# Layer 0's last head pair: the root by POOL's power, value copies on ScalarE, and rows turned only between two tiles of a projection job

## The chip, the cores and the metric

The kernel runs on one NeuronCore of a Trainium2 chip. The metric is the time of one execution on the device in microseconds (us). A core has five engines with instruction streams of their own: TensorE (PE) for matmuls and transposes, with its weight loads shown apart as PEld; VectorE (DVE); ScalarE (ACT), whose functions come from tables that are loaded when they change; GpSimd (POOL); and SyncE (SP), which here issues the DMA transfers. Each engine takes its instructions strictly in order and waits on semaphores for the others. On-chip memory is SBUF, and PSUM for the results of matmuls.

## The reference

Two layers over N = 4096 nodes with 512 features, 8 heads of 64, in float32. Layer 0 is graph attention with additive scores, layer 1 attention with dot products:

```python
h = relu(layernorm(x))                       # layer 0
d1 = (h @ W.T + b).reshape(N, 8, 64)
src, trg = (d1 * src_proj).sum(-1), (d1 * trg_proj).sum(-1)
e = leaky(src.T[:, :, None] + trg.T[:, None, :]) + adj     # slope 0.01
x = x + (softmax(e) @ d1 per head)
h = relu(layernorm(x))                       # layer 1
k, q, v = h @ Wks, h @ Wqs, h @ Wvs          # per head
s = q @ k.T / 8 - 1e16 * (1 - max(adj, eye))
x = x + sum over heads of softmax(s) @ v @ Wo
```

The layer norm of layer 1 needs all 512 features of a row, and so the sums of all of layer 0's heads.

## The kernel before, in words

The program has three stages. Stage A does the first three head pairs of layer 0 with tiles of 128 rows by 4096 columns. Stage B, from about 1717 us to 2529 us of the span, does the last pair. Stage C is layer 1. The change touches stage B alone, apart from one constant (`neghalf`) made at the start.

Stage B works in **slots**, the loop over `s` at its end. A slot handles 32 rows by 4096 columns for both heads of the pair, laid out as 128 partitions by 1024 columns for each head: a partition holds one row and a quarter of the columns. Four slots (`GS`) make a **group** of 128 rows, and there are 32 groups, so 128 slots. Two groups (`BR`) make a **block** of 256 rows. The order of the instructions on each engine is the order of the program, since the stage stands under `manual_schedule`. For one slot's data the steps are spread over several passes of the loop:

- the adjacency rows are loaded three slots ahead by SP (L586, four DMAs of 128 KB);
- `leaky(s+1)` (L599, ACT): source plus target score through the leaky function, into one of two PSUM buffers per head tile (`lk`);
- `masked(s)` (L609, DVE, twice): adds the adjacency, writes the negated sum to the SBUF ring `t` and takes the row's smallest value. The ring has 12 slots (`RING`), so three groups;
- `parted` (L616, POOL) and, in every even slot, `smallest` (L625 on PE into the single PSUM buffer `ms`, L630 on DVE): the smallest values of a row's four quarters brought together;
- `exps(s-3)` (L641, ACT, twice): the exponentials with their sums;
- `squares(s-4)` (L648, DVE): transposes 32x32 squares in place;
- `weighted(s-8)` (L656, PE, 32 matmuls, here called the output pass): sums a quarter of the columns times the values d1 for all four slots of a group into the PSUM tile `bo`. Four such passes finish a group.

A group's results then pass through `finish`, a generator that is advanced once per slot: den (L672, PE) and its reciprocal (L676, DVE) in one slot, back (L680, PE, transposing the group's output that ACT copied with L665) and batt (L682, DVE) two slots later, then the addition to the residual row tile on POOL (L686), the statistics on DVE (L690, L694), and for every second group the root on ACT (L700), its reciprocal on DVE (L702), the normalisation on POOL (L706), and the transposes of the two row tiles on PE (L716, called turns), each with its relu on DVE (L717). The finished block is handed to `projected`, a **job**: queries and keys for layer 1, four PSUM tiles copied out by ACT (L733), and values, two PSUM tiles copied out by DVE (L745); each copy goes to HBM through SP.

In detail, a job has 32 query and key units, eight for each of the four tiles, and eight value units, four for each of the two tiles; in PE's timeline a unit is two matmul instructions. `work` runs in each slot and spends `UNITS` credits on the job at the head of the list: a query or key unit counts one, a value unit two, so that a job costs 48. PE's order in a slot is: `work`, `smallest` (even slots), the steps of `finish`, the output pass. ACT's is: copy of a finished group's output (first slot of a group), leaky, exponentials, then the copies of `work`. DVE's is: two masks, squares, what `work` gives it, the minima, the steps of `finish`.

Three bounds tie the engines together. The tiles of the turns and of the projections share one PSUM pool of two buffers (tag `mp`): a tile can begin when the one before the last has been copied out. The ring `t` lets the masks of a group's first slot start only when the output pass of the slot just before it is done. And the output pass of a group's first slot needs the squares of that group's last slot.

After the last slot the remaining jobs run on alone; this part is called the tail. Stage C starts with the keys and values that the jobs wrote.

Of the kernel before, what the change touches and what calls it, by code (L numbers as in the profile page):

```python
# [8 lines left out]
F32 = mybir.dt.float32  # L9
AF = mybir.ActivationFunctionType  # L10
ALU = mybir.AluOpType
# [4 lines left out]
P = 128  # L16
EPS = 1e-5
# [6 lines left out]
def kernel(  # L24
# [14 lines left out]
    nc = tc.nc  # L39
    N, DM = x.shape  # L40
    H, D = src_proj.shape[1:]
    HD = H * D
    NB = N // P
    KC = DM // P
# [6 lines left out]
    const = ctx.enter_context(tc.tile_pool(name="const", bufs=1))  # L51
    dram = ctx.enter_context(tc.tile_pool(name="dram", bufs=1, space=DRAM))

    ident = const.tile([P, P], F32, name="ident")
    make_identity(nc, ident)
    eps = const.tile([P, 1], F32, name="eps")
    nc.gpsimd.memset(eps, EPS)


    SQ = 32  # L60
    NS = P // SQ
    band = const.tile([P, SQ], F32, name="band")
# [36 lines left out]
    with tc.tile_pool(name="a0k", bufs=1) as pk, tc.tile_pool(name="a0v", bufs=4) as pv, tc.tile_pool(  # L99
        name="a0a", bufs=3  # L100
    ) as pa, tc.tile_pool(name="a0t", bufs=6) as pt, tc.tile_pool(name="a0p", bufs=4) as pp, tc.tile_pool(
        name="a0x", bufs=1
    ) as px, tc.tile_pool(name="a0h", bufs=3) as ph, tc.tile_pool(name="a0s", bufs=4) as psb, tc.tile_pool(
        name="a0tr", bufs=3, space=PSUM
# [200 lines left out]
        hTs = [None]  # L305
# [119 lines left out]
        def step(n):  # L425
            return groups[n // 2], n % 2

        with tc.manual_schedule():
# [45 lines left out]
            for s in range(total + 6):  # L474
                G, h = step(s) if s < total else (None, 0)
                for half in range(2):
# [4 lines left out]
                    turn = 0 <= n < 2 * total  # L481
                    if turn:
                        T, i = groups[n // HALVES], n % HALVES
# [43 lines left out]
    RING = 12  # L527
    EXPS, TURN, PROD = 3, 4, 8
    BR = 2
    UNITS = 6  # L530
    with tc.tile_pool(name="b0c", bufs=1) as pc, tc.tile_pool(name="b0a", bufs=4) as pa, tc.tile_pool(
        name="b0w", bufs=1
    ) as pk, tc.tile_pool(name="b0t", bufs=1) as pt, tc.tile_pool(name="b0v", bufs=GS) as pv, tc.tile_pool(
        name="b0x", bufs=6
    ) as pxr, tc.tile_pool(name="b0h", bufs=4) as ph, tc.tile_pool(name="b0e", bufs=4) as pe, tc.tile_pool(
        name="b0ht", bufs=2
    ) as phT, tc.tile_pool(
        name="b0s", bufs=6
    ) as psb, tc.tile_pool(name="b0o", bufs=1) as px, tc.tile_pool(
        name="b0lk", bufs=2, space=PSUM  # L540
    ) as plk, tc.tile_pool(name="b0m", bufs=1, space=PSUM) as pm, tc.tile_pool(
        name="b0po", bufs=1, space=PSUM
# [124 lines left out]
        def finish(G):  # L667

            yield
            den = pm.tile([P, P], F32, tag="ms", name="den")  # L670
            for k in range(GS):
                nc.tensor.matmul(  # L672
                    den[bass.ts(k, SQ), :2], lhsT=band, rhs=G.sm[:, k, :], start=True, stop=True
                )
            rden = psb.tile([P, 2], F32, name="rden")
            nc.vector.reciprocal(rden, den[:, :2])  # L676
            yield
            yield
            back = pm.tile([P, P], F32, tag="ms", name="back")
            nc.tensor.transpose(back, G.oT, ident)  # L680
            att = px.tile([P, 2, D], F32, name="batt")
            nc.vector.tensor_mul(  # L682
                att, back.rearrange("p (h d) -> p h d", d=D), rden.unsqueeze(2).to_broadcast([P, 2, D])
            )
            last = G.x[:, C3 * PR :]
            nc.gpsimd.tensor_add(last, last, att.rearrange("p h d -> p (h d)"))  # L686
            nc.sync.dma_start(x1_d[bass.ts(G.g, P), C3 * PR :], last)
            yield
            stats = psb.tile([P, 6], F32, name="bstats")
            nc.vector.bn_stats(stats, G.x)  # L690
            if G.g % BR == 0:
                block[0] = psb.tile([P, BR, 2], F32, name="bmv")
            mv = block[0]
            nc.vector.bn_aggr(mv[:, G.g % BR], stats)  # L694
            if G.g % BR < BR - 1:
                return
            Gs = groups[G.g - BR + 1 : G.g + 1]
            yield
            rstd = psb.tile([P, BR, 1], F32, name="brstd")
            nc.scalar.activation(rstd, mv[:, :, 1:2], AF.Sqrt, bias=eps)  # L700
            yield
            nc.vector.reciprocal(rstd, rstd)  # L702
            hns = []
            for j in range(BR):
                hn = ph.tile([P, DM], F32, name="bhn")
                nc.gpsimd.tensor_scalar(  # L706
                    hn, Gs[j].x, mv[:, j, 0:1], rstd[:, j], ALU.subtract, ALU.mult
                )
                hns.append(hn)
            yield  # L710
            hT = phT.tile([P, KC, BR * P], F32, name="bhT")
            for j in range(BR):
                yield
                tp = pmm.tile([P, KC, P], F32, tag="mp", name="tp")
                for kc in range(KC):
                    nc.tensor.transpose(tp[:, kc, :], hns[j][:, bass.ts(kc, P)], ident)  # L716
                nc.vector.tensor_scalar(hT[:, :, bass.ts(j, P)], tp, 0.0, None, ALU.max)  # L717
            jobs.append(projected(Gs, hT))

        def projected(Gs, hT):  # L720

            rows = bass.ts(Gs[0].g // BR, BR * P)
            for c in range(HC):
                mp = pmm.tile([P, 2, BR * P], F32, tag="mp", name="mp")
                for i, w in ((0, wk), (1, wq)):
                    for kc in range(KC):
                        nc.tensor.matmul(
                            mp[:, i], lhsT=w[:, kc, bass.ts(c, P)], rhs=hT[:, kc, :],
                            start=(kc == 0), stop=(kc == KC - 1),
                        )  # L730
                        if (i, kc) == (1, KC - 1):
                            e = pe.tile([P, 2, BR * P], F32, name="e")
                            nc.scalar.copy(e, mp)  # L733
                            nc.sync.dma_start(qk_d[:, c, :, rows], e)
                        yield 1
            for j in range(BR):
                mp = pmm.tile([P, 512], F32, tag="mp", name="mpv")
                for kc in range(KC):
                    nc.tensor.matmul(
                        mp, lhsT=hT[:, kc, bass.ts(j, P)], rhs=wv[:, kc, :],  # L740
                        start=(kc == 0), stop=(kc == KC - 1),
                    )
                    if kc == KC - 1:
                        e = pe.tile([P, 512], F32, name="e")
                        nc.vector.tensor_copy(e, mp)  # L745
                        nc.sync.dma_start(v_d[bass.ts(Gs[j].g, P), :], e)
                    yield 2

        groups = [Rows(g) for g in range(NG)]
        block = [None]  # L750
        jobs = []

        def step(n):
            return groups[n // GS], n % GS

        def work():

            units = 0
            while jobs and units < UNITS:
                try:  # L760
                    units += next(jobs[0])
                except StopIteration:
                    jobs.pop(0)

        with tc.manual_schedule():
# [4 lines left out]
            for s in range(SETS + PROD + 10):  # L770
# [23 lines left out]
                if s % 2 and s < SETS:  # L794
                    G, k = step(s)
# [3 lines left out]
                if s % 2 == 0 and 0 <= s - 2 < SETS:  # L799
                    G, k = step(s - 2)  # L800
# [3 lines left out]
                if 0 <= n < SETS:  # L804
                    W, w = step(n)
                    weighted(W, w)
                    if w == GS - 1:
                        endings = [*endings[-2:], finish(W)]
            while jobs:
                work()  # L810
    l0.close()
    att_d = dram.tile([HC, P, N], F32, name="att_d")
# [17 lines left out]
    with tc.tile_pool(name="a1t", bufs=1) as pt, tc.tile_pool(name="a1k", bufs=4) as pkk, tc.tile_pool(  # L830
        name="a1v", bufs=GS
    ) as pv, tc.tile_pool(name="a1a", bufs=6) as pa, tc.tile_pool(name="a1q", bufs=2) as pq, tc.tile_pool(
        name="a1x", bufs=2
    ) as px, tc.tile_pool(name="a1s", bufs=6) as psb, tc.tile_pool(name="a1z", bufs=2) as pz, tc.tile_pool(name="a1at", bufs=3) as pat, tc.tile_pool(
        name="a1sc", bufs=4, space=PSUM
    ) as psc, tc.tile_pool(name="a1tr", bufs=1, space=PSUM) as ptr, tc.tile_pool(
        name="a1m", bufs=1, space=PSUM
# [271 lines left out]
        with tc.manual_schedule():  # L1109
# [18 lines left out]
            for s in range(total + PROD + 3):  # L1128
# [11 lines left out]
                turn = 0 <= s - TURN < total  # L1140
                if turn:
                    squares(*step(s - TURN))
                turn = turn and (s - TURN) % 2
# [3 lines left out]
                if s % 2 and 0 <= s - 3 < total:  # L1147
                    G, k = step(s - 3)
# [16 lines left out]
                if s % 2 and s < total:  # L1165
                    G, k = step(s)
# [46 lines left out]
```

## Time and profile before

| What | Value |
|---|---|
| Median of 3 runs | 4940.27 us (4938.2 to 4942.55) |
| Profiled execution, time | 4940.09 us |
| Profiled execution, span of the core | 4938.3 us |
| Mean granted TensorE clock | 0.98 of full |
| PE, DVE, ACT, POOL busy over the span | 96%, 90%, 78%, 9% |
| Stage B: first leaky, last matmul of the last job ends | 1723.1 us, 2528.9 us |
| One mask (L609), one squares (L648), in ns | 1215, 2307 |
| One leaky (L599), one exponential (L641), in ns | 1113, 1135 |
| Copies L733 (ACT) and L745 (DVE), in ns | 563, 655 |
| Table load, in ns | 1283 |

The span runs from the first to the last instruction of the profiled execution; its time has 1.8 us more around it. In the profile a group of instructions has a line of the kernel, an engine, an operation, and the tiles that it writes and reads. "Idle before" is the time that the engine stood still ahead of these instructions, with what ended it. A releaser is inferred: where the one named had long been done, it was another. A timeline line gives the start in us from the span's start, the length, the engine, the line, and in brackets the wait ahead of it.

### The profile page before, as it was taken

How to read it: one execution, taken by the hardware profiler on the slowest of the kernel's cores; microseconds unless marked ns; L12 is line 12 of the kernel's file. 1: busy time of each engine (PE TensorE's matmuls, PEld its weight loads, DVE VectorE, ACT ScalarE, POOL GpSimd, SP SyncE). 2: the span in 40 equal slices, each digit the busy share in tenths (PEclk: the TensorE clock that was granted, in tenths of full speed). 3: DMA queues.
4: the chain of work that ended last, by engine and by line, in shares of the span. 5: the costliest groups of instructions: out<-in, count | busy, mean ns of one | idle time of the engine just before them, and what ended most of it. 6: DMA issues, size and time to landing. Idle time of an engine off the chain costs nothing.

```text
span 4938.3 us, 144474 instructions
## 1 busy us (share of the span) xinstructions
PE 4719.5 (96%) x61554; PEld 3518.5 (71%) x61554; DVE 4462.5 (90%) x7841; ACT 3857.6 (78%) x4301; POOL 459.2 (9%) x932
## 2 busy tenths in 40 slices
PE   6999999999999958989989999999999999999998
PEld 5888888888888847767756666666666666666664
DVE  4999999999999898888749999999999999999981
ACT  4999999999999899888748888766666666666660
POOL 2000000000000011111123333100000000000000
PEclk8999999999999979999999999999999999999999
DMA  6444454445444384444367787633445343534435
GB/s 233 158 152 157 162 193 161 152 153 206 153 156 158 115 181 135 143 140 135 111 192 249 241 265 237 223 130 131 152 152 170 130 156 129 189 129 136 158 124 192
DMA packets 358838, 819.44 MB, mean 166 GB/s; under 512 B 60080, under 2 KB 179120, under 8 KB 333104
## 3 DMA queue, kind: packets, MB, share of 16 engines
q1 hardware_dynamic: 358192, 810.21, 50.0%
q8 instruction: 481, 7.88, 0.6%
q14 instruction: 165, 1.35, 0.1%
HBM read 669.26 MB, written 140.77 MB: 164 GB/s over the span
## 4 chain that ended last, share of the span: by engine, by line
PE 57%; ACT 15%; DVE 15%; issue 8%; DMA 3%; SPq 1%; POOL 0%; DVEq 0%; ACTq 0%; POOLq 0%
PE sc L920 20%; PE o L1004 20%; ACT t L168 6%; PE tr L986 5%; DVE t L158 5%; DVE pT L192 4%; ACT t L147 4%; DVE bt L609 3%; PE tr L181 3%; PE o L203 3%; ACT pT L190 2%; PE oo L1087 2%; ACT bt L641 2%; DVE bt L648 2%; DMA ba<-in_adj_dram 1%
## 5 line engine op out<-in xcount | busy, mean ns | idle before, releaser
L936 DVE CUSTOM_DVE_ANT_0 t<-sc,a 128x512 f32<-128x512 f32 x2048 | 1285.7, 683 | 99.3 <-PE sc L920 52.0
L971 ACT ACTIVATE t<-t,nm 128x1024 f32<-128x1024 f32 x1024 | 1165.9, 1142 | 103.1 <-DVE nm L960 103.0
L1004 PEld LDWEIGHTS o<-t,v 128*64 128x64 f32 x16384 | 883.8, 137 | 429.4 <-issue 321.2
L920 PE MATMUL sc<-k,q 64*32 64x512 f32 x16384 | 1028.1, 597 | 10.5 <-DVE nm L936 10.4
L1004 PE MATMUL o<-t,v 128*64 128x128 f32 x16384 | 1007.4, 276 | 0.4 <-ACT oT L1013 0.4
L158 DVE CUSTOM_DVE_ANT_0 t<-t,a 128x2048 f32<-128x2048 f32 x384 | 876.0, 2281 | 41.2 <-ACT t L147 41.0
L978 DVE STREAM_TRANSPOSE t<-t 128x1536 f32<-128x1536 f32 x512 | 908.2, 1774 | 1.1 <-ACT t L971 1.1
L181 PE MATMUL tr<-ident,t 128*128 128x128 f32 x6144 | 781.5, 278 | 34.1 <-ACT pT L190 20.1
L203 PE MATMUL o<-pT,v 128*64 128x128 f32 x12288 | 756.8, 276 | 1.0 <-DVE pT L192 0.8
L181 PEld LDWEIGHTS tr<-ident,t 128*128 128x128 f32 x6144 | 665.4, 141 | 125.9 <-issue 65.3
L147 ACT ACTIVATE t<-tb,src 128x4096 f32<-128x4096 f32 x192 | 730.1, 3803 | 18.7 <-DMA tb<-trg_d 18.7
L168 ACT ACTIVATE t<-t,nm 128x4096 f32<-128x4096 f32 x192 | 729.8, 3801 | 8.5 <-DVE nm L163 8.4
L203 PEld LDWEIGHTS o<-pT,v 128*64 128x64 f32 x12288 | 664.0, 137 | 61.3 <-issue 46.8
L993 ACT COPY t<-tr 128x1024 f32<-128x1024 f32 x256 | 259.1, 1012 | 515.9 <-PE tr L986 507.0
L192 DVE COPY pT<-tr 128x1024 f32<-128x1024 f32 x549 | 652.5, 1213 | 9.8 <-PE tr L181 9.8
L920 PEld LDWEIGHTS sc<-k,q 64*32 64x32 f32 x16384 | 259.4, 106 | 371.8 <-issue 215.5
L599 ACT ACTIVATE lk<-tb,srcb 128x1024 f32<-128x1024 f32 x256 | 282.3, 1113 | 82.3 <-DVE nm L609 75.0
L609 DVE CUSTOM_DVE_ANT_0 bt<-lk,ba 128x1024 f32<-128x1024 f32 x256 | 302.0, 1215 | 24.8 <-ACT e L733 12.7
L648 DVE STREAM_TRANSPOSE bt<-bt 128x2048 f32<-128x2048 f32 x128 | 295.2, 2307 | 29.0 <-ACT bt L641 29.0
L641 ACT ACTIVATE bt<-bt,nm 128x1024 f32<-128x1024 f32 x256 | 290.3, 1135 | 0.4 <-DVE nm L630 0.3
L656 PE MATMUL bo<-bt,bv 128*64 128x128 f32 x4096 | 282.8, 297 | 5.9 <-ACT boT L665 4.5
L986 PE MATMUL tr<-ident,t 128*128 128x128 f32 x2048 | 280.8, 280 | 0.8 <-ACT t L971 0.7
(115 smaller groups left out, 3750.5 us busy)
## 6 DMA issues: line engine op xcount, KB each, us to landing
a<-in_adj_dram SPq DMA_DIRECT2D x192, 1024.0 KB
a<-pen_d SPq DMA_DIRECT2D x384, 512.0 KB
ba<-in_adj_dram SPq DMA_DIRECT2D x512, 128.0 KB
a<-in_adj_dram SPq DMA_DIRECT2D x512, 128.0 KB
pen_d<-a SPq DMA_DIRECT2D x128, 512.0 KB
h<-hT_d SPq DMA_DIRECT2D x96, 256.0 KB
qk_d<-e SPq DMA_DIRECT2D x64, 256.0 KB
x<-in_x_dram SPq DMA_DIRECT2D x8, 1024.0 KB
```

The source lines that it names most:

```text
L147: nc.scalar.activation(t, targets[G.c, h], AF.Prelu, bias=src[:, G.g, 2 * G.c + h : 2 * G.c + h + 1], alpha=SLOPE)
L158: nc.vector.tensor_tensor_reduce(out=t, in0=t, in1=rows_of_adj[G, f], scale=-1.0, scalar=FMAX, op0=ALU.add, op1=ALU.min, accum_out=nm[:, f ...
L168: nc.scalar.activation(G.t[h], G.t[h], AF.Exp, bias=G.nm[h][:, NCH : NCH + 1], scale=-1.0, accum_out=G.sm[:, h : h + 1],)
L181: nc.tensor.transpose(tr[:, bass.ts(b % 4 * 2 + h, P)], G.t[h][:, bass.ts(i * MB + b, P)], ident)
L192: nc.vector.tensor_copy(pT, tr)
L203: nc.tensor.matmul(G.o[h * D : (h + 1) * D, :P], lhsT=feats[G.c][i][:, b, bass.ts(h, D)], rhs=pT[:, bass.ts(b % 4 * 2 + h, P)], start=(mb ...
L920: nc.tensor.matmul(sc[h][bass.ts(a, SQ), :], lhsT=G.q[bass.ts(h, D), bass.ds(G.q0 + k * SQ, SQ)], rhs=keys[G.c][half][bass.ts(h, D), a, :] ...
L936: nc.vector.tensor_tensor_reduce(out=t[:, G.ring + k, h, cols], in0=scs[half][h], in1=a[:, cols], scale=1.0, scalar=FMAX, op0=ALU.add, op1 ...
L971: nc.scalar.activation(u, u, AF.Exp, bias=G.nm[k // 2][:, k % 2, h : h + 1], scale=-1.0, accum_out=G.sm[:, h, k : k + 1],)
L978: nc.vector.transpose(u, u)
L986: nc.tensor.transpose(tr[:, j, h, bass.ts(m, P)], t[:, G.ring + k - 1 + j, h, bass.ds(VC + m * P, P)], ident,)
L1004: nc.tensor.matmul(G.o[bass.ts(h, D), :P], lhsT=v[:, b, bass.ts(h, D)], rhs=t[:, bass.ds(G.ring, GS), h, bass.ds(at, SQ)], start=(mb == 0) ...
```

## The change

Six things change in stage B. The root of the variance plus eps is taken on POOL as a power of -0.5 (`neghalf`), with a shift worked out beside it, in place of ACT's Sqrt and DVE's reciprocal, and the normalisation is a multiplication and an addition. The value copies move from DVE to ACT. `den` and `back` share one PSUM tile and come in the same slot, two slots earlier than `back` before. The statistics, the root and the normalisation follow in the next slot. The turns leave `finish`: they stand in a list, and `work` takes one from it only when the job at the head stands between two tiles and fewer than two jobs are listed; after a turn, `work` does no more in that slot. `UNITS` is 7 in place of 6, and credits that a slot leaves are kept, up to 9 in hand.

```diff
--- before.py
+++ after.py
@@ -55,6 +55,8 @@
     make_identity(nc, ident)
     eps = const.tile([P, 1], F32, name="eps")
     nc.gpsimd.memset(eps, EPS)
+    neghalf = const.tile([P, 1], F32, name="neghalf")
+    nc.gpsimd.memset(neghalf, -0.5)
 
 
     SQ = 32
@@ -527,7 +529,7 @@
     RING = 12
     EXPS, TURN, PROD = 3, 4, 8
     BR = 2
-    UNITS = 6
+    UNITS = 7
     with tc.tile_pool(name="b0c", bufs=1) as pc, tc.tile_pool(name="b0a", bufs=4) as pa, tc.tile_pool(
         name="b0w", bufs=1
     ) as pk, tc.tile_pool(name="b0t", bufs=1) as pt, tc.tile_pool(name="b0v", bufs=GS) as pv, tc.tile_pool(
@@ -667,20 +669,17 @@
         def finish(G):
 
             yield
-            den = pm.tile([P, P], F32, tag="ms", name="den")
+            ms = pm.tile([P, 2, P], F32, tag="ms", name="back")
             for k in range(GS):
                 nc.tensor.matmul(
-                    den[bass.ts(k, SQ), :2], lhsT=band, rhs=G.sm[:, k, :], start=True, stop=True
-                )
+                    ms[bass.ts(k, SQ), 1, :2], lhsT=band, rhs=G.sm[:, k, :], start=True, stop=True
+                )
+            nc.tensor.transpose(ms[:, 0], G.oT, ident)
             rden = psb.tile([P, 2], F32, name="rden")
-            nc.vector.reciprocal(rden, den[:, :2])
-            yield
-            yield
-            back = pm.tile([P, P], F32, tag="ms", name="back")
-            nc.tensor.transpose(back, G.oT, ident)
+            nc.vector.reciprocal(rden, ms[:, 1, :2])
             att = px.tile([P, 2, D], F32, name="batt")
             nc.vector.tensor_mul(
-                att, back.rearrange("p (h d) -> p h d", d=D), rden.unsqueeze(2).to_broadcast([P, 2, D])
+                att, ms[:, 0].rearrange("p (h d) -> p h d", d=D), rden.unsqueeze(2).to_broadcast([P, 2, D])
             )
             last = G.x[:, C3 * PR :]
             nc.gpsimd.tensor_add(last, last, att.rearrange("p h d -> p (h d)"))
@@ -695,29 +694,38 @@
             if G.g % BR < BR - 1:
                 return
             Gs = groups[G.g - BR + 1 : G.g + 1]
-            yield
+
             rstd = psb.tile([P, BR, 1], F32, name="brstd")
-            nc.scalar.activation(rstd, mv[:, :, 1:2], AF.Sqrt, bias=eps)
-            yield
-            nc.vector.reciprocal(rstd, rstd)
+            nc.gpsimd.tensor_scalar(rstd, mv[:, :, 1:2], 1.0, EPS, ALU.mult, ALU.add)
+            nc.gpsimd.tensor_tensor(rstd, rstd, neghalf.unsqueeze(1).to_broadcast([P, BR, 1]), ALU.pow)
+            shift = psb.tile([P, BR, 1], F32, name="bshift")
+            nc.gpsimd.tensor_mul(shift, mv[:, :, 0:1], rstd)
+            nc.gpsimd.tensor_scalar(shift, shift, -1.0, 0.0, ALU.mult, ALU.add)
             hns = []
             for j in range(BR):
                 hn = ph.tile([P, DM], F32, name="bhn")
-                nc.gpsimd.tensor_scalar(
-                    hn, Gs[j].x, mv[:, j, 0:1], rstd[:, j], ALU.subtract, ALU.mult
-                )
+                nc.gpsimd.tensor_scalar(hn, Gs[j].x, rstd[:, j], shift[:, j], ALU.mult, ALU.add)
                 hns.append(hn)
             yield
-            hT = phT.tile([P, KC, BR * P], F32, name="bhT")
-            for j in range(BR):
-                yield
+            yield
+            hTs = []
+
+            def turn(j):
+                if j == 0:
+                    hTs.append(phT.tile([P, KC, BR * P], F32, name="bhT"))
+                hT = hTs[0]
                 tp = pmm.tile([P, KC, P], F32, tag="mp", name="tp")
                 for kc in range(KC):
                     nc.tensor.transpose(tp[:, kc, :], hns[j][:, bass.ts(kc, P)], ident)
                 nc.vector.tensor_scalar(hT[:, :, bass.ts(j, P)], tp, 0.0, None, ALU.max)
-            jobs.append(projected(Gs, hT))
+                if j == BR - 1:
+                    jobs.append(projected(Gs, hT))
+
+            for j in range(BR):
+                turns.append((turn, j))
 
         def projected(Gs, hT):
+
 
             rows = bass.ts(Gs[0].g // BR, BR * P)
             for c in range(HC):
@@ -732,7 +740,7 @@
                             e = pe.tile([P, 2, BR * P], F32, name="e")
                             nc.scalar.copy(e, mp)
                             nc.sync.dma_start(qk_d[:, c, :, rows], e)
-                        yield 1
+                        yield 1, (i, kc) == (1, KC - 1)
             for j in range(BR):
                 mp = pmm.tile([P, 512], F32, tag="mp", name="mpv")
                 for kc in range(KC):
@@ -742,23 +750,34 @@
                     )
                     if kc == KC - 1:
                         e = pe.tile([P, 512], F32, name="e")
-                        nc.vector.tensor_copy(e, mp)
+                        nc.scalar.copy(e, mp)
                         nc.sync.dma_start(v_d[bass.ts(Gs[j].g, P), :], e)
-                    yield 2
+                    yield 2, kc == KC - 1
 
         groups = [Rows(g) for g in range(NG)]
         block = [None]
         jobs = []
+        turns = []
+        credit = [0]
+        whole = [True]
 
         def step(n):
             return groups[n // GS], n % GS
 
         def work():
 
-            units = 0
-            while jobs and units < UNITS:
+
+            credit[0] = min(credit[0] + UNITS, UNITS + 2)
+            while credit[0] > 0:
+                if turns and whole[0] and len(jobs) < 2:
+                    turn, j = turns.pop(0)
+                    turn(j)
+                    return
+                if not jobs:
+                    return
                 try:
-                    units += next(jobs[0])
+                    units, whole[0] = next(jobs[0])
+                    credit[0] -= units
                 except StopIteration:
                     jobs.pop(0)
 
@@ -806,7 +825,7 @@
                     weighted(W, w)
                     if w == GS - 1:
                         endings = [*endings[-2:], finish(W)]
-            while jobs:
+            while jobs or turns:
                 work()
     l0.close()
     att_d = dram.tile([HC, P, N], F32, name="att_d")
```

## The prediction

> **What bounds the kernel now.** The edit lies in layer 0's last head pair (1.72 to 2.53 ms of the span), so I read the page's 40 slices for where that is and then only views of that stretch. DVE's timeline gives the start of each slot's first mask (L609). With s mod 8 as the slot's number, slot 0 of s = 40 starts at 1924.46 us and that of s = 120 at 2391.01: ten cycles of eight slots (two row groups, one job) in 466.55 us, 46.66 us each. First the busy times of that stretch and of the tail, from the last masks to the last projection (columns: length, then busy us and instructions of PE, weight loads, DVE, ACT, POOL; clock; DMA share; GB/s):
>
> ```profile
> 1924.46:2391.01 466.55, 424.71 (x3700) 333.48 (x3700) 413.17 (x571) 409.04 (x571) 58.87 (x80) 0.93 0.46 139
> ...
> 2433.80:2529.00 95.20, 91.22 (x603) 66.29 (x609) 24.82 (x36) 22.24 (x40) 13.80 (x13) 1.00 0.28 98
> ```
>
> Three engines at 88 to 91%: PE 42.5, DVE 41.3, ACT 40.9 of 46.66 us per cycle. None fills it, so the waits matter (total us, times, longest, over the ten cycles):
>
> ```profile
> PE mpv L739 <- DVE nm L609: 26.8, 9, 3.0
> DVE bt L648 <- ACT bt L641: 21.0, 10, 2.1
> ...
> PE tp L716 <- DVE e L745: 12.0, 10, 1.5
> DVE bhT L717 <- PE tp L716: 11.3, 10, 1.1
> DVE bt L609 <- ACT e L733: 11.1, 7, 1.6
> ```
>
> Each comes once per cycle. The timeline of PE round one of them shows what they cost:
>
> ```profile
> 2061.81 1.98 PE L739 MATMUL mpv<-wv,bhT 128*128 128x512 f32 x4
> 2066.77 1.12 PE L739 MATMUL mpv<-wv,bhT 128*128 128x512 f32 x2 [2.98 <-DVE nm L609]
> 2067.73 0.35 PE L625 MATMUL nmB<-parts,bands 128*128 128x16 f32 x2
> 2069.57 1.11 PE L716 MATMUL tp<-ident,bhn 128*128 128x128 f32 x4 [1.49 <-DVE e L745]
> 2070.61 3.68 PE L656 MATMUL bo<-bt,bv 128*64 128x128 f32 x32
> 2074.23 3.03 PE L739 MATMUL mpv<-wv,bhT 128*128 128x512 f32 x6
> 2077.10 0.60 PE L716 MATMUL tp<-ident,bhn 128*128 128x128 f32 x4
> 2077.63 0.24 PE L672 MATMUL den<-bsm,band 128*32 128x2 f32 x8
> 2077.80 1.97 PE L656 MATMUL bo<-bt,bv 128*64 128x128 f32 x32
> 2079.70 1.99 PE L727 MATMUL mp<-bhT,wk 128*128 128x256 f32 x8
> ```
>
> The second value tile needs one of two "mp" PSUM buffers, whose key/query copy (L733) ACT finishes at 2066.71; the release named, DVE, had long been done. ACT is late because of two table loads in the two slots before it. Then L716 turns rows in the middle of a job and waits for the value copy (L745) behind DVE's masks and squares; DVE in turn waits for L716. After the gap PE runs cold: the output pass L656 takes 3.68 instead of 1.97 us. From 2077.80 on PE is back to back for most of a cycle.
>
> PE's work warm, from start to start: output pass 1.90 us (2077.80 to 2079.70); a query/key unit 0.448 (six in 2.69); a value unit 0.86 (two in 1.72); a turned tile 0.53; nmB 0.22; den and back 0.37. A cycle is 8 x 1.90 + 32 x 0.448 + 8 x 0.86 + 2 x 0.53 + 4 x 0.22 + 2 x 0.37 = 39.1. With 4.5 of gaps, 3.1 is left for the cold clock: 46.7. That closes, so PE's order with its two gaps sets the cycle. DVE feels it: the ring t has 12 slots, so the mask of a group's first slot waits for the output pass of the slot just before (the 1.6 us waits above).
>
> **What the skill says.** The Trainium skill, "ScalarE: Activation LUTs", What ACT_TABLE_LOAD costs, gives 1283 ns plus a drain of some 1380 ns per switch. The trace has 1283 ns, but the next instruction starts within 0.02 us; I use 1.28. "TensorE: Matmul & The Clock Gate", Part 1, says that an idle window of about 3.4 us halves the clock until a busy one has passed; 3.68 against 1.97 us after a gap of 2.98 agrees. "GPSIMD Engine Reference", 3.1, gives two-input elementwise about 2.6 cycles per element plus dispatch; no page prices a power on POOL.
>
> **The change, part by part**, per cycle.
>
> *Square root to POOL.* ACT loses two loads and a Sqrt (2 x 1.28 + 0.30); DVE loses the reciprocal L702 (0.145). POOL gains four ops on 128x2: the nearest row, parts 128x16, is 0.218, so 0.9 in all; the power is not in the trace, 0.1 to some 5 us, I take 0.25. The new normalisation has the form of L338, not of L706 (POOL's groups over the whole span: busy, mean ns of one, idle before):
>
> ```profile
> L706 POOL TENSOR_SCALAR bhn<-xr,bmv,brstd 128x512 f32<-128x512 f32 x32 | 66.2, 2077 | 110.8 <-issue 87.3 <-DVE brstd L702 23.5
> ...
> L338 POOL TENSOR_SCALAR hn<-x,rstd,shift 128x512 f32<-128x512 f32 x32 | 24.3, 774 | 40.9 <-DVE shift L331 23.0 <-PE htp L350 13.5 <-DMA trg_d<-lr 4.5
> ```
>
> Two of them fall from 4.15 to 1.55 us. POOL is 13% busy, and rows are turned three slots later, so all of it is hidden. Queued behind it is parts (L616), hence nmB, the minima and the exponentials: see the third rival.
>
> *Value copies to ACT.* DVE loses 2 x 0.665, ACT gains 2 x 0.563 (the L733 row, same shape). The copies stand ahead of the next slot's leaky; DVE needs that leaky more than 2 us later, so a copy of 0.56 is taken up, and four in a row (slots 2 to 5) too, since DVE itself waits ahead of slot 4. DVE: 41.3 - 1.33 - 0.145 = 39.8. ACT: 40.9 - 2.86 + 1.13 = 39.2. The v_d writes on SP now wait for ACT; the adjacency loads queued behind them run three slots ahead, which covers about 2 us of lateness.
>
> *A constant.* One memset of 128x1 at the start, 0.10 by the row of eps, ahead of work that waits for loads: nothing.
>
> *den and back together.* Same matmuls and DVE ops, back two slots earlier, one wait on the single "ms" buffer less; nothing on the path.
>
> *Order of the projection.* Counting credits (7 a slot, at most 9 in hand, a turn ends the slot's work): slot 7 has 9 query/key units, slots 0, 1, 2 seven each, 3 has two and three value units, 4 three value units, 5 two and turn 0, 6 only turn 1. The total is the same; jobs start three slots earlier.
>
> PE by slot, output pass included: slot 7 5.93, 0 5.26, 1 5.41, 2 5.26, 3 5.38: 27.2 us back to back. Then the ring: slot 4's mask waits for slot 3's output pass (0.1 to hand over). From that mask DVE needs 4.57 (slot 4), 5.5 (slot 5, 4.5 plus relu 0.68, rden, batt) and 5.2 (slot 6 to the end of its relu): 15.3. PE has only 11.9 us for slots 4 to 6; in it turn 1 waits about 2 us for ACT's second value copy (leaky and exponentials 4.5 a slot, copy 0.56), which is hidden. The next job's first matmul needs that relu, 0.05 later. Cycle: 27.2 + 0.1 + 15.3 + 0.05 = 42.7. I add 0.5: gaps of 2 and 1 us stand close together, and a cold window (3.4 us at half speed, 1.7 lost) may fall in one cycle of three. 43.2. DVE's own 39.8 leaves it about 3.4 idle, mostly ahead of slot 4.
>
> *Tail.* Before, from the last slot 7's mask (2431.41) to the last value matmul (2528.94): 97.5. After, PE starts the next slot 5.0 after that mask (its slot 7 begins 0.95 ahead of the mask, since slot 6's relu ends at 5.2 of DVE's 6.15 us there, and takes 5.93), with 87 query/key units left instead of 96, 24 value units instead of 30 and 4 turns instead of 6: 87 x 0.448 + 24 x 0.86 + 8 x 1.90 + 4 x 0.53 + 1.3 (nmB, den, back) + 1.3 (one copy, one relu to wait for) = 79.6, so 84.6 to 85. Gain 12.5.
>
> *Sum.* s = 24 to 32: 42.77 to 43.2, loss 0.4. 32 to 40: 45.82 to 43.2, gain 2.6. Ten cycles: 466.55 to 432, gain 34.6. Slot 0 to slot 7 of the last: 40.40 to 38.2, gain 2.2. Tail 12.5. Together 51.5. Span 4938.3 - 51.5 = 4886.8; 1.8 lie around it, and the median of the runs is 0.2 above the profiled run: 4889 us.
>
> **The rivals.** (1) The clock goes on falling once per cycle: 1.7 lost in each, so 44.4; gain 10 x 2.26 + 1.4 + 1.0 - 1.6 + 12.5 = 36, 4904. For: the gap of 2 us at turn 1, and early in the stage a gap of 2.21 us is followed by a 3.46 us output pass. Against: gaps of 1.0 and 1.4 there are followed by 1.97. (2) The slots smooth out more than I think and DVE's 39.8 is near the bound: 41.5 a cycle; gain 10 x 5.16 + 4.3 + 3.8 + 1.3 + 12.5 = 73, 4867. Against: the hand-overs at slots 4 and 7 follow from the ring and the tile. (3) Slower: POOL's power is a slow routine of X us. Parts of slot 3 stands behind it, and the next nmB in slot 4. POOL is free at about 7.6 + X after slot 2's start; PE wants parts 14 after. Up to X = 6 nothing; beyond, each us adds one to each of 16 cycles, and the gain of 3.5 a cycle is gone at X = 9.5 and the tail's with it above 10.3: slower from there, and by 16 x 1.5 - 12.5 = 11.5 at X = 11, 4952. Against: two elements per partition, and every short POOL row is under 0.5 us. (4) The bunched slots cost what the waits did (four copies in a row on ACT, 9 units ahead of the ring's wait): 46 a cycle, 10 x 0.66 - 3.4 + 12.5 = 16, 4925. Against: ACT's slots with copies are 5.1 and two before and two after have none.
>
> **Chances.** Forecast 0.50, rival 1 0.24, rival 2 0.12, rival 4 0.11, rival 3 0.03. The forecast's own range is 4880 to 4897; with rival 1 whole, and parts of 2 and 4, 4866 to 4912. A change of 0.2% (10 us) is about what can be told from none here: faster 0.95, same 0.02, slower 0.03.
>
> **What would show it.** No table load between 1.73 and 2.53 ms; PE's wait at L739 gone; turn 1's transposes waiting some 2 us for a value copy in slot 6; masks of s = 4 mod 8 about 2 us late, the others not; masks eight slots apart by 43 us; clock 0.97 or more in the stage; last projection 51 us earlier; POOL's normalisation at 0.77 us; layer 1 unchanged. Wrong if the power takes several us, if the clock stays at 0.93, or if ACT's copies hold PE at the second value tile as before.

## The result

| | before | after |
|---|---|---|
| Median of the runs, us | 4939.24 (4 runs, 4937.67 to 4942.55) | 4913.10 (4 runs, 4911.99 to 4913.65) |
| Ratio after / before, 95% | | 0.9946 [0.9929, 0.9963] |
| Profiled execution: time, span, us | 4940.09, 4938.3 | 4913.65, 4911.9 |
| Cycle of eight slots, s = 40 to 120, us | 46.66 | 45.05 |
| Last slot 7's mask to the end of stage B, us | 97.5 | 88.1 |
| Stage C, us | 2409.4 | 2409.2 |

The change gains 26 us, half of the 51.5 forecast. The time is 1 us above the range's upper end of 4912. Of the span's gain of 26.4 us the ten cycles bring 16.1 (466.55 to 450.48; forecast 34.6) and the tail 9.4 (forecast 12.5). Slots 0 to 24 lose 1.2, 24 to 32 lose 1.9, 32 to 40 gain 1.3, and the slots 120 to 127 gain 2.6. Stage C, 4911.9 less the 2502.7 at which the last value matmul of stage B ends, is what it was within 0.2.

First the busy times of the same two stretches as before, the ten cycles and the tail (columns: length, then busy us and instructions of PE, weight loads, DVE, ACT, POOL; clock; DMA share; GB/s), of the kernel after:

```profile
1926.31:2376.79 450.48, 417.27 (x3701) 326.59 (x3701) 402.86 (x541) 392.72 (x561) 45.69 (x120) 0.95 0.48 144
2416.00:2504.00 88.00, 86.84 (x601) 63.99 (x599) 18.78 (x25) 19.77 (x36) 9.00 (x20) 0.98 0.28 95
```

DVE's 40.3 and ACT's 39.3 us a cycle are near the 39.8 and 39.2 that were worked out. (Warm stands below for matmuls at the full granted clock, cold for those at half of it.) The surprise is the clock: 0.95, where 0.97 or more was the mark, and 0.98 in a tail that ran at 1.00 before. The waits of the ten cycles (total us, times, longest):

```profile
ACT lk L601 <- DVE nm L611: 44.1, 50, 1.6
DVE bt L611 <- ACT e L741: 39.6, 19, 2.4
...
PE mp L735 <- DVE nm L632: 28.7, 10, 2.9
...
ACT boT L667 <- PE bo L658: 11.0, 21, 1.8
...
PE tp L719 <- DVE bhT L720: 4.5, 10, 0.5
```

Of the waits shown before, the one at the second value tile (26.8 us) and that of a turn for the value copy (12.0) are gone. In their place PE has one wait of 2.9 us per cycle at L735, the first matmul of a job in slot 7, and 0.45 at the second turn. PE's timeline round it, in the cycle from 2011 us on:

```profile
2046.24 1.97 PE L658 MATMUL bo<-bt,bv 128*64 128x128 f32 x32
2048.66 0.66 PE L719 MATMUL tp<-ident,bhn 128*128 128x128 f32 x4 [0.46 <-DVE bhT L720]
2049.15 0.37 PE L627 MATMUL nmB<-parts,bands 128*128 128x16 f32 x2
2049.45 1.97 PE L658 MATMUL bo<-bt,bv 128*64 128x128 f32 x32
2054.28 3.35 PE L735 MATMUL mp<-bhT,wk 128*128 128x256 f32 x8 [2.87 <-DVE nm L632]
2057.43 2.23 PE L735 MATMUL mp<-bhT,wq 128*128 128x256 f32 x8
2059.50 0.59 PE L735 MATMUL mp<-bhT,wk 128*128 128x256 f32 x2
2060.02 1.97 PE L658 MATMUL bo<-bt,bv 128*64 128x128 f32 x32
```

After the gap of 2.87 us the same eight instructions that take 1.97 us elsewhere take 3.35, and the next eight 2.23: slot 7's nine units need 5.74 us from 2054.28 to 2060.02 where the warm price gives 4.03. The release named, L632, is not the one: DVE's timeline in that slot shows what the job waits for.

```profile
2038.85 1.23 DVE L611 CUSTOM_DVE_ANT_0 bt<-lk,ba 128x1024 f32<-128x1024 f32 x1 [1.86 <-ACT e L741]
...
2051.26 2.31 DVE L650 STREAM_TRANSPOSE bt<-bt 128x2048 f32<-128x2048 f32 x1
2053.49 0.65 DVE L720 TENSOR_SCALAR bhT<-tp 128x512 f32<-128x512 f32 x1
2054.06 0.16 DVE L632 TENSOR_REDUCE nm<-nmB 128x4 f32<-128x16 f32 x1
```

The first line is slot 4's mask, 1.86 us late for the output pass as forecast. The second relu (L720) ends at 2054.14, 15.3 us after it as forecast, and the job starts 0.14 later. Its transposes on PE had been done since 2049.3; the relu stood behind slot 6's squares (2.31 us) on DVE.

On POOL the new normalisation and the power (groups over the span: busy, mean ns of one, idle before):

```profile
L707 POOL TENSOR_SCALAR bhn<-xr,brstd,bshift 128x512 f32<-128x512 f32 x32 | 24.5, 773 | 1.7
L700 POOL TENSOR_TENSOR brstd<-brstd,neghalf 128x2 f32<-128x2 f32 x16 | 11.3, 704 | 1.3
```

### The profile page after: what moved, and what is told of

It reads as the page before. It is cut to its first block, busy times and chain, and to the rows that moved or that the text cites. A ratio compares the mean times of both kernels' runs of the same rounds, so it can differ in the third digit from the quotient of the medians.

```text
span 4911.9 us, 144507 instructions
## 1 busy us (share of the span) xinstructions
PE 4707.5 (96%) x61554; PEld 3506.2 (71%) x61554; DVE 4446.0 (91%) x7793; ACT 3833.3 (78%) x4287; POOL 438.3 (9%) x997
## 4 chain that ended last, share of the span: by engine, by line
PE 61%; DVE 17%; ACT 11%; issue 7%; DMA 3%; SPq 1%; POOL 0%; DVEq 0%; ACTq 0%; POOLq 0%
PE sc L939 20%; PE o L1023 20%; DVE t L160 7%; PE tr L1005 5%; PE mp L735 5%; DVE pT L194 5%; ACT t L170 5%; ACT t L149 3%; PE bo L658 2%; PE tr L183 2%; PE o L205 2%; DVE bt L611 2%; PE oo L1106 2%; ACT pT L192 2%; DVE bt L650 2%
## 5 line engine op out<-in xcount | busy, mean ns | idle before, releaser
L149 ACT ACTIVATE t<-tb,src 128x4096 f32<-128x4096 f32 x192 | 726.1, 3782 | 18.5 <-DMA tb<-trg_d 18.5
L658 PE MATMUL bo<-bt,bv 128*64 128x128 f32 x4096 | 257.6, 280 | 8.9 <-ACT boT L667 7.6
```

The lines of the kernel that those rows point to most:

```text
L149: nc.scalar.activation(t, targets[G.c, h], AF.Prelu, bias=src[:, G.g, 2 * G.c + h : 2 * G.c + h + 1], alpha=SLOPE)
```

## The experiments

Theory: the chain of waits is as forecast and would give a cycle of about 43, and the clock, which falls after the one gap in nearly every cycle, makes it 45. Rival: the chain itself is longer, and the cold stretch is hidden in it. A second question is what each part is worth, since the two moves of work were priced by engine totals only. Cycle is the mean of the ten from s = 40 to 120. Only `e1_warm` and `e6_warm_half` do more work than the kernel after, in idle transposes; none leaves any out.

| Kernel | Median, us | Ratio to before [95%] | Cycle, us |
|---|---|---|---|
| after | 4913.10 | 0.9946 [0.9929, 0.9963] | 45.05 |
| e1_warm | 4891.91 | 0.9902 [0.9887, 0.9917] | 43.15 |
| e6_warm_half | 4892.62 | 0.9904 [0.9884, 0.9924] | 43.32 |
| e2_relu_early | 4870.25 | 0.9858 [0.9844, 0.9873] | 41.80 |
| e3_copies_dve | 4911.26 | 0.9937 [0.9920, 0.9954] | 44.28 |
| e4_root_act | 4907.77 | 0.9935 [0.9920, 0.9950] | 44.33 |
| o1_order_only | 4912.16 | 0.9940 [0.9925, 0.9954] | 44.74 |
| b1_root_pool | 4898.55 | 0.9912 [0.9897, 0.9927] | 43.39 |
| b2_copies_act | 4964.73 | 1.0045 [1.0028, 1.0062] | 48.52 |
| b3_root_copies | 4924.57 | 0.9965 [0.9952, 0.9978] | 45.51 |
| b4_root_squares_late | 4881.43 | 0.9880 [0.9865, 0.9895] | 41.73 |
| e7_early_copies_dve | 4884.85 | 0.9888 [0.9872, 0.9905] | 42.88 |
| e8_early_root_act | 4905.75 | 0.9931 [0.9916, 0.9945] | 44.25 |

### Filling the gap: is it the clock?

`e1_warm` is the kernel after with 18 transposes of the identity, whose result nobody reads, behind slot 6's output pass:

```diff
+                    if w == 2 and W.g % 2 and W.g > 2 and s < SETS:
+                        warm = pmm.tile([P, KC, P], F32, tag="mp", name="warm")
+                        for _ in range(18):
+                            nc.tensor.transpose(warm[:, 0, :], ident, ident)
```

> The changed kernel with 18 extra identity transposes on PE (about 2.4 us, into a spare mp tile that nothing reads) after the output pass of every slot 6, where PE stands idle for 2.87 us. Theory C (the clock falls in that gap, so the first units of slot 7 run at half speed): the gap shrinks to about 0.5, the nine units of slot 7 take 4.0 instead of 5.7 us, the cycle falls from 44.8 to 43.0, time about 4888 us. Rival R (the first matmuls of a job are slow for another reason, such as reading rows just written while DVE and ACT use SBUF): slot 7 stays at 5.7 us, cycle 44.8, 4913 us. Output is that of the reference.

PE's timeline at the same place of `e1_warm`:

```profile
2045.84 2.18 PE L829 MATMUL warm<-ident 128*128 128x128 f32 x18
2048.78 1.97 PE L735 MATMUL mp<-bhT,wk 128*128 128x256 f32 x8 [0.75 <-DVE nm L632]
2050.58 1.89 PE L735 MATMUL mp<-bhT,wq 128*128 128x256 f32 x8
```

The job starts no earlier in its cycle (15.43 us after slot 4's mask in both kernels), but warm, 1.97 and 1.89 us. All ten cycles are 43.15, the stage's clock is 1.00, and the kernel is 21 us faster though it does more. The theory holds. The span's gain over before is 45.8 us in the profiled execution, which is the slowest of four, and 49.2 by the medians, against the 51.5 forecast.

`e6_warm_half` has 9 of the transposes:

```diff
-                        for _ in range(18):
+                        for _ in range(9):
```

> The changed kernel with 9 extra identity transposes instead of 18 after the output pass of slot 6: of the gap about 1.75 us are left. If what makes the clock fall is idle time gathered in one stretch of some us, this gap is too short: slot 7 warm, cycle 43.1, 4891 us, as with 18. If any gap ahead of slot 7 does it: cycle 44.8, 4913 us. In between (some cycles cold): 4898 to 4905 us.

The gap that is left is 1.73 us, in PE's timeline:

```profile
2045.90 1.97 PE L735 MATMUL mp<-bhT,wk 128*128 128x256 f32 x8 [1.73 <-DVE nm L632]
```

Nine of ten cycles are 43.15 and one is 44.84, which is 43.15 and the 1.7 of a cold window. Half the filling is nearly enough.

### Closing the gap: the relu ahead of the squares

`e2_relu_early` is the kernel after with the squares issued behind `work`:

```diff
-                if 0 <= s - TURN < SETS:
-                    squares(*step(s - TURN))
                 ...
                 work()
+                if 0 <= s - TURN < SETS:
+                    squares(*step(s - TURN))
```

> The changed kernel with DVE's squares put after what work() issues, so that the relu of a turned tile stands ahead of the squares of its slot instead of behind them; nothing else moves. Theory C with the chain that I worked out (slot 4's mask waits for slot 3's output pass, DVE's slots 4 to 6 up to the second relu, then slot 7): the relu comes 2.2 us earlier, the gap ahead of slot 7 shrinks to about 0.6 us, the clock stays up, and DVE (40.5 us of work by its slots) becomes the bound: cycle 40.7 to 41.5, time about 4866 us. Rival R: gap gone but slot 7 stays slow, cycle 42.6, 4885 us. If the relu is not what slot 7 waits for: 4913 us.

DVE's timeline in slot 6 of `e2_relu_early`, and PE's at the job's start:

```profile
2078.48 0.69 DVE L720 TENSOR_SCALAR bhT<-tp 128x512 f32<-128x512 f32 x1
2079.08 2.30 DVE L650 STREAM_TRANSPOSE bt<-bt 128x2048 f32<-128x2048 f32 x1
```

```profile
2079.31 1.97 PE L735 MATMUL mp<-bhT,wk 128*128 128x256 f32 x8 [0.67 <-DVE bhT L720]
```

The relu now goes first, the gap is 0.67 us, the matmuls are warm. The cycle is 41.80 us, a little over the 40.7 to 41.5 expected. This also shortens the chain, and so gives more than warmth alone: now DVE is nearly the bound, busy 96% of the stage:

```profile
1926.00:2350.00 424.00, 408.54 (x3758) 317.27 (x3757) 407.95 (x550) 392.69 (x569) 46.27 (x122) 1.00 0.54 156
```

At 4870.25 us, 1.4% below before, it is the fastest of all kernels here.

### Each part undone, with the new order kept

`e3_copies_dve` puts the value copies back on DVE, `e4_root_act` the root back on ACT with the reciprocal on DVE a slot later, `o1_order_only` undoes both. The normalisation keeps its new form in all three.

```diff
-                        nc.scalar.copy(e, mp)
+                        nc.vector.tensor_copy(e, mp)
```

```diff
-            nc.gpsimd.tensor_scalar(rstd, mv[:, :, 1:2], 1.0, EPS, ALU.mult, ALU.add)
-            nc.gpsimd.tensor_tensor(rstd, rstd, neghalf.unsqueeze(1).to_broadcast([P, BR, 1]), ALU.pow)
+            nc.scalar.activation(rstd, mv[:, :, 1:2], AF.Sqrt, bias=eps)
+            yield
+            nc.vector.reciprocal(rstd, rstd)
             ...
-            yield
```

> The changed kernel with the value copies back on DVE (one part undone). They then stand in slots 4 and 5 of DVE, between slot 4's mask and the second relu, which is the path by theory C: cycle 44.8 plus 1.3 = 46.1, time about 4930 us. If DVE is not on the path there (rival: PE alone bounds the cycle): 4913 us.

> The changed kernel with the root back on ACT (Sqrt, two table loads per cycle) and its reciprocal on DVE one slot later; turns in the same slots. ACT is 2.9 us later in slots 3 and 4. By theory C PE has slack of 2.9 us from slot 4 to slot 7, so only the exponentials that squares need in slot 5 are late, by about 1 us: cycle 45.5 to 46.5, time 4920 to 4933 us. If the table loads were the main cost before: cycle 47.5 or more, 4945 us.

> The changed kernel with both engine moves undone: root on ACT with its table loads, value copies on DVE. What is left of the change is the order alone (turns between tiles, credits, den and back together). Theory C: DVE's path from slot 4 to the second relu is 1.2 longer, the table loads fall into PE's slack, and the gap ahead of slot 7 is colder or warmer by its place: cycle 44.3 to 45.5, time 4908 to 4925 us, so that the order alone brings nearly the whole gain. Rival P (each part brings its share): the order brings a third of 26 us at most, 4930 us or more.

The first two were missed. By the intervals of their ratios neither can be told from the kernel after, where 7 to 20 us more had been expected. In `e3_copies_dve` DVE's slots 4 and 5 are the expected 1.2 us longer together (5.18 and 6.12 instead of 4.58 and 5.52 us), but in all ten cycles the job starts warm, in four of them after a gap hardly shorter than the kernel after has (PE's timeline):

```profile
2054.53 1.99 PE L735 MATMUL mp<-bhT,wk 128*128 128x256 f32 x8 [2.78 <-DVE bhT L720]
```

In the other six the output pass ahead of the gap is cold and fills a part of it, so that 1.1 to 1.6 us are left; the job starts 16.53 us after slot 4's mask in all ten. What DVE loses, the clock gives back: the cycle of 44.28 us is the warm chain of 43.15 with those 1.2. In `e4_root_act` ACT's lateness shows up at the second value tile, and what PE waits there is taken out of the gap ahead of the job. Three places in its PE timeline, the gap in two successive cycles and the value tile:

```profile
2007.57 3.65 PE L735 MATMUL mp<-bhT,wk 128*128 128x256 f32 x8 [2.03 <-DVE nm L632]
...
2052.40 1.97 PE L735 MATMUL mp<-bhT,wk 128*128 128x256 f32 x8 [2.03 <-DVE nm L632]
...
2082.21 1.98 PE L747 MATMUL mpv<-wv,bhT 128*128 128x512 f32 x4 [1.16 <-ACT e L741]
```

The gap is now 2.03 us, and the same 2.03 is followed once by 3.65 and once by 1.97. Seven of the ten cycles are 44.84 us long and three 43.14. `o1_order_only` came as expected. The new order of the projection brings the whole gain of the change, and the two moves of work add nothing that can be measured to it.

Why equal gaps end differently is to be read from the granted clock that the trace records. In every kernel it changes only at the ticks of a fixed grid of 3.413 us; a window is the stretch from one tick to the next. Cut along that grid, the two gaps of `e4_root_act` look so (columns as in the stretches above; PE's busy time and the clock count):

```profile
2004.27:2007.68 3.41, 1.38 (x25) 1.17 (x22) 3.41 (x6) 3.41 (x5) 0.00 (x0) 1.00 0.70 216
2007.68:2011.09 3.41, 3.41 (x9) 2.69 (x10) 3.31 (x7) 2.08 (x4) 0.18 (x1) 0.50 0.81 192
...
2048.64:2052.05 3.41, 1.73 (x32) 1.49 (x28) 3.41 (x4) 3.41 (x6) 0.00 (x0) 1.00 0.57 184
2052.05:2055.46 3.41, 3.06 (x14) 2.75 (x15) 3.31 (x7) 2.10 (x3) 0.00 (x0) 1.00 0.84 221
```

The first gap lies whole in one window, 2.03 of 3.41 us idle, and the window after it runs at half clock. The second is split by a tick into 1.68 and 0.35, and the clock stays. A cycle of 44.84 is 13 windows and 0.46 us, so the gap moves along the grid until a tick splits it. A cycle of 44.28, in `e3_copies_dve` and in most cycles of `o1_order_only`, is 13 windows less 0.09: the gap of 2.78 hardly moves, and in the former's line above a tick splits it into 1.40 and 1.38 (at 2053.15), in the latter so that less than 2.0 is in one window in eight cycles of ten. In the kernel after all ten gaps have 2.1 us or more in one window. So the misses go back to how the gaps lie against the grid. This is read from the traces: no run moved a gap along the grid and left all else alone.

### Each part alone, in the old order

`b1_root_pool` is the kernel before with the root and the normalisation's new form on POOL, `b2_copies_act` with the value copies on ACT, `b3_root_copies` with both; the edits are the lines of the change.

> The kernel before with the root alone moved to POOL (same slots, same order, normalisation as multiplication and addition). Both table loads go, so ACT's copy of the last key/query tile is in time and the wait of 2.98 at the second value tile goes; the turn in slot 0 still waits for DVE's value copy, by then 2.3 us after PE is ready. My working: PE 39.1 plus that gap plus what is cold after it, cycle 42 to 44.5, time 4885 to 4915 us. Rival P (a share of the gain): about 4931 us.

> The kernel before with the value copies alone moved to ACT. The turn in slot 0 then waits for a copy that stands behind ACT's leaky and exponentials of that slot instead of behind DVE's masks and squares, some 2 us later, and the gap is colder: cycle 48 to 49, time 4955 to 4970 us, slower than before. Rival P (DVE is relieved by 1.3 per cycle): 4925 us.

> The kernel before with both engine moves and the old order (turns in the middle of a job). The table loads are gone, but the turn in slot 0 waits for ACT's copy at the end of that slot, about 3.6 us after PE is ready, and the clock falls there: cycle 45 to 46.5, time 4915 to 4938 us. Rival P: both moves bring 17 us or more, 4922 us, and the order the rest.

All three came within what was expected. PE's timeline of `b1_root_pool`: the wait at the second value tile is gone, and one at the turn is left, 2.29 us, after which the output pass is cold in seven cycles of ten:

```profile
2053.99 0.98 PE L719 MATMUL tp<-ident,bhn 128*128 128x128 f32 x4 [2.29 <-DVE e L748]
2054.90 3.26 PE L658 MATMUL bo<-bt,bv 128*64 128x128 f32 x32
```

PE's timeline of `b2_copies_act`, where both waits stand, the second longer than before, because the copy now stands behind that slot's leaky and exponentials on ACT (the copy starts at 2081.28 in this cycle) instead of behind DVE's squares. The table loads are not needed for it: `b3_root_copies`, which has none, waits 3.73 us at this place.

```profile
2076.92 2.07 PE L739 MATMUL mpv<-wv,bhT 128*128 128x512 f32 x2 [2.98 <-DVE nm L609]
...
2081.91 1.12 PE L716 MATMUL tp<-ident,bhn 128*128 128x128 f32 x4 [2.67 <-ACT e L745]
2082.95 3.63 PE L656 MATMUL bo<-bt,bv 128*64 128x128 f32 x32
```

In the old order the root, with the normalisation's new form (not run apart from it), is worth 43 us (0.9912), the copies cost 22 (1.0045), and the root alone is better than the whole change. The effects don't add up: the order alone brings 30 us, the root alone 43, all three together 26.

### The parts once the gap is closed

`e7_early_copies_dve` and `e8_early_root_act` undo the same parts in `e2_relu_early`; `b4_root_squares_late` is `b1_root_pool`, with the old order, and its squares behind `work`.

> The changed kernel with the early relu of the second experiment (squares after work()) and the value copies back on DVE. The slack that hid this part is gone, DVE is the bound there with a wait of 1.2 us ahead of slot 4 that the copies can't use: cycle 41.8 plus 1.2 = 43.0, time 4886 us. Rival (the place of the copies never matters): 4870 us.

> The changed kernel with the early relu and the root back on ACT. ACT's 2.9 us of loads and Sqrt no longer fall into a gap of PE: the second value tile waits 1 us, squares wait for late exponentials: cycle 43 to 44, time 4886 to 4900 us. Rival (the root never matters in the new order): 4870 us.

> The kernel before, old order, with the root on POOL and DVE's squares put after what work() issues, so that the value copy stands ahead of the slot's squares. Theory C: the gap of 2.29 us at the turn goes and with it the cold clock; PE's 39.1 and DVE's 41.1 of work are left: cycle 41.5, time about 4874 us, so the new order of the projection is not needed for the gain. Rival O (turns inside a job cost by themselves): cycle 43 or more, 4893 us or more.

Now the moves count: the copies 14.6 us, as expected, the root 35.5, more than expected. PE's timeline of `e8_early_root_act` at the second value tile shows why: the wait that the gap absorbed in `e4_root_act` is on the path, and the job starts 15.71 us after slot 4's mask in place of 13.43.

```profile
2040.22 1.98 PE L747 MATMUL mpv<-wv,bhT 128*128 128x512 f32 x4 [2.01 <-ACT e L741]
```

`b4_root_squares_late` has cycles as short as `e2_relu_early` (41.73 and 41.80), with the old order and the value copies on DVE. Its time is 7 us over the 4874 expected. The 11 us between the two lie in the tail, from the last slot 7's mask to the end of the stage: 96.3 us in the former, 82.9 in the latter. With the gap closed, a shorter tail is all that the new order with its copies on ACT still brings.

## Why the prediction missed

**Right.** The chain: the masks of slot 4 wait 1.86 us (about 2 forecast), DVE's path from there to the second relu is 15.3, POOL's normalisation 0.773 (0.774), the wait at the second value tile is gone, there is no table load in the stage, stage C is unchanged. The power took 0.704 us, where 0.25 was taken out of 0.1 to 5, and is hidden as argued; the third rival falls with it.

**The step that failed** is "I add 0.5: gaps of 2 and 1 us stand close together, and a cold window (3.4 us at half speed, 1.7 lost) may fall in one cycle of three", and with it the wait that it rests on, "turn 1 waits about 2 us for ACT's second value copy". Turn 1 doesn't wait for that copy. In each of the ten cycles its transposes start 0.05 us after the first turn's relu ends and 0.75 before the copy begins; DVE's and ACT's timelines in the cycle shown above, where turn 1 starts at 2048.66:

```profile
2047.95 0.66 DVE L720 TENSOR_SCALAR bhT<-tp 128x512 f32<-128x512 f32 x1
```

```profile
2049.41 0.56 ACT L753 COPY e<-mpv 128x512 f32<-128x512 f32 x1
```

The second value tile still holds its PSUM buffer then, so turn 1 stands in the buffer that turn 0 left. That a tile of this pool can begin only when the one before the last has been copied out doesn't hold here. The wait is 0.45 us, where the copy, which ends at 2049.97, would have made it 1.8. So PE's idle time in slots 4 to 6 is not divided: nearly all of it comes in one piece of 2.87 us ahead of slot 7, and slot 7 stands on the path with nothing to hide behind. The clock fell in every one of the ten cycles.

Warm, the chain is 43.15 us (`e1_warm`), made of 27.5 for PE from slot 7 to slot 3, 0.2 to the mask, 15.3, and 0.15 to the job, where 27.2, 0.1, 15.3 and 0.05 gave 42.7. So the 43.2 that I forecast was a figure for a clock that never falls; the 0.5 was used up by small terms. With the clock most cycles are 44.83 (1.7 lost), two are 46.15 (3.0 lost) and two 44.6 (1.4 lost). The guess of one cycle in three had no rule behind it for when the clock falls; the prediction's own figures nearest to 2.87, gaps of 2.98 and 2.21 us, were both followed by a cold output pass, though both are shorter than the idle window of about 3.4 us with which it took the first to agree. The cold clock costs 450.48 - 431.5 = 19.0 us in the ten cycles, and their shortfall is 34.6 - 16.1 = 18.5.

**The tail** fell short by the same cause. After the last gap of 2.87 us the clock stayed low until 2419.92, for nearly all of the nine units. PE's timeline of the kernel after:

```profile
2413.79 3.75 PE L735 MATMUL mp<-bhT,wk 128*128 128x256 f32 x8 [2.87 <-DVE nm L632]
2417.33 3.17 PE L735 MATMUL mp<-bhT,wq 128*128 128x256 f32 x8
2420.35 0.59 PE L735 MATMUL mp<-bhT,wk 128*128 128x256 f32 x2
```

They take 7.08 us from 2413.79 to 2420.87 instead of 4.03. Along the grid, the kernel after has two cold windows here, because the first of them still holds the end of the gap:

```profile
2409.68:2413.09 3.41, 1.24 (x24) 1.00 (x20) 3.41 (x6) 3.33 (x5) 0.00 (x0) 1.00 0.27 96
2413.09:2416.51 3.42, 2.72 (x7) 2.20 (x8) 3.32 (x7) 3.42 (x7) 0.00 (x0) 0.50 0.02 5
2416.51:2419.92 3.41, 3.41 (x10) 2.66 (x9) 3.41 (x4) 0.05 (x1) 0.22 (x1) 0.50 0.00 0
```

Without these 3.05 the tail would be 85.0, where 84.6 to 85 was forecast; `e1_warm`, warm there, has 85.1. The two cycles from s = 24 to 40 fall short by 1.5 and 1.3 more. That is the clock too: they take 44.68 and 44.53 in the kernel after, and 43.15 and 43.14 in `e1_warm`. The 1.2 us lost before s = 24 I didn't trace; the slots 120 to 127 make up for 0.4.

**The rivals.** The first, the clock falling once per cycle, named the mechanism, and its 4904 was 9 us too low: it took 1.7 for every cycle, on a chain 0.45 too short, and nothing in the tail. Its place for the gap, turn 1, was the wrong one. Its evidence against itself, gaps of 1.0 and 1.4 us that stayed warm, was about shorter gaps than this one. The second rival's cycle of 41.5 is what `e2_relu_early` comes near to. The fourth, bunched slots, had a nearby size (46) for a reason that doesn't hold: the same bunched slots take 43.15 with the gap filled.

**The pricing of the two moves** by totals of ACT and DVE was right in the totals and says nothing of time: in this order what ACT or DVE loses is taken out of PE's gap or given back by the clock, and undoing either move changed the time by nothing measurable.

## What to carry to other kernels

When PE has idle time that can't be removed, ask where in the cycle it gathers, not only how much it is: a gap of 2.87 us ahead of work on the path cost another 1.4 to 3.0 us of cold clock, and filling it with idle transposes took that away. On an in-order engine, look at what stands ahead of a short operation that another engine waits for; moving the relu ahead of one 2.3 us transpose was worth more (43 us) than the whole change (26). And price a part of a change in the order in which it will run: the value copies were worth nothing, gained 14.6 us or cost 22, and the root was worth nothing, 35.5 or 43, according to where the slack was.

## What the runs showed of the hardware that was not expected

The clock goes by windows, not by gaps. The Trainium skill, "TensorE: Matmul & The Clock Gate", Part 1, says that the activity window of 3413 ns runs freely; the recorded clock agrees, since all its changes in a run lie on one grid of 3.413 us. The page asks for an idle window; here much less is enough. Over the windows of 450 us of the stage in all 14 traces, by PE's idle time in a warm window:

| Idle in a warm window | Windows | Next window cold |
|---|---|---|
| under 1.4 us | 1627 | 0 |
| 1.4 to 2.0 us | 55 | 9 |
| 2.0 us and more | 56 | 56 |

A cold window with less than 0.5 us idle was followed by a warm one in 64 of 64, one with more by another cold one in 30 of 32. In the kernel before, ahead of these windows, a gap of 2.46 us is split by a tick at 1845.96 into 1.20 and 1.26, and the eight matmuls behind it take a warm 1.99. What decides between 1.4 and 2.0 us these runs don't show (PE's ends are modelled, and some matmul records can be missing). A cold window that falls into slack costs nothing: in six cycles of `e3_copies_dve` the output pass ahead of the gap is the cold one (3.2 to 3.6 us for 1.97), and the job behind the gap starts no later.

POOL's tensor-scalar of 128x512 takes 2.08 us as subtract and multiply and 0.77 as multiply and add, in the same stage; in `b1_root_pool`, in the same slots as before, it is 0.77 too.
